# GRU recurrence: the work behind the z gate done by halves of the features

## The chip, the cores and the metric

The kernel runs on one core of a Trainium2 chip. A core has five engines with queues of their own: PE (TensorE, matrix products; the profile lists its weight loads apart, as PEld), DVE (VectorE), ACT (ScalarE), POOL (GpSimd) and SP (SyncE, which here only issues DMAs). They are kept in step by semaphores. The metric is the device time of one launch in microseconds (us).

## The reference

`x` has the shape (16, 256, 512): 16 batches, 256 channels, 512 positions. `cond` has the shape (16, 512) and holds zeros and ones. Four stages each add their result to `x`:

1. attention over the 512 positions, masked by `cond` (8 heads),
2. a causal convolution along the channels: the 16 rows of `cond` are its 16 taps, one value per tap and feature,
3. a GRU that walks over the 256 channels as its time steps, with 512 features and `cond` as the first state,
4. a second masked attention (16 heads).

The change lies in stage 3. One time step of it is

```python
def cell(h, x):
    gi = x @ W_ih + b_ih
    gh = h @ W_hh + b_hh
    i_r, i_z, i_n = jnp.split(gi, 3, axis=-1)
    h_r, h_z, h_n = jnp.split(gh, 3, axis=-1)
    r = jax.nn.sigmoid(i_r + h_r)
    z = jax.nn.sigmoid(i_z + h_z)
    n = jnp.tanh(i_n + r * h_n)
    h_new = (1.0 - z) * n + z * h
    return (h_new, h_new)
```

Each step needs the state of the step before it, so the 256 steps can't be reordered. The kernel computes the last line as `h + (1 - z) * (n - h)`.

## The kernel before

All data are fp32. `P` is 128, `B` is 16 (batches), `D` is 256 (time steps here) and `T` is 512 (features), so `NT = T // P` is 4 blocks of 128 features. The first attention ends with its sums in `xT` (128 features on the partitions, then 4 blocks, 16 batches, 256 steps), and the last attention begins when the recurrence has ended.

**State.** The new state of each step is kept in `hist`, two tiles of 16 steps each, laid out as 128 partitions x step x 4 blocks x 32. Of the 32 columns one step fills 16, even steps one half and odd steps the other; the rest is zero. `state(t)` (L1036) gives the part that a step writes and the whole slot that the next step's products read.

**Products.** `state_part` (L1080) multiplies the state by the hidden weights `whh` for one gate: for each block `f` of 128 input features, outermost, four products that stand side by side on four groups of 32 PE columns. Each product reads `slot[:, f]`, the state of one block. The profile shows 32 matmul records for one call, eight for each `f`. The input's share of r and z (`input_part`, L1058) is accumulated into the same PSUM tiles ahead of time, two steps at once, and the input's share of n is made by `turned_part` (L1066) into `turned`. PSUM holds two sets of `pr`, `pn`, `pz`; a set serves two steps and then gets the biases copied in again (L1164, ACT).

**One step** (`step`, L1094) is a chain over three engines. PE makes `pr`; ACT takes the sigmoid (`r`, L1108); DVE transposes it in blocks of 32 x 32 (`rT`, L1109), which brings the features onto the partitions. PE makes `pn`; DVE transposes that (`hT`, L1111), multiplies (`rn`, L1112) and adds the input's share (`pre`, L1113). PE makes `pz`; ACT takes the tanh of `pre` (`nn`, L1115); DVE transposes `pz` (`zT`, L1116); ACT makes `1 - z` from it (`omz`, L1117, sigmoid with scale -1); DVE makes `d = nn - h` (L1118), `m = d * omz` (L1119) and the new state `m + h` (L1120, written to `hist`). `mine` picks the 16 of 32 columns that belong to this step. A transposed tile has 128 columns: 4 blocks of 32, so its first 64 columns belong to blocks 0 and 1.

**Order of the work.** The whole recurrence is emitted in program order under a manual schedule (L1132): every engine executes its instructions in the order in which the Python lines emit them, and the framework adds the semaphores. Behind each `step(t)` the loop at L1156 emits, in this order: four input products (PE), in odd steps the three bias copies (ACT), one piece of `turned_part` (PE, with an ACT instruction in every fourth), in four steps of sixteen a copy `xw` (L1056, ACT), and two pieces of other work on DVE. The latter are convolution products for later steps (`conv`, L533) or, twice at the start of each sixteen steps, `add_part` (L1092), which adds finished states to `xT`. So on DVE two pieces of this work stand between the new state and the next step's `rT`; on PE input products stand between `pz` and the next step's `pr`.

Of the kernel before, what the change touches and what calls it, by code (L numbers as in the profile page):

```python
# [11 lines left out]
AF = mybir.ActivationFunctionType  # L12
ALU = mybir.AluOpType
# [3 lines left out]
P = 128  # L17
# [233 lines left out]
def tile_kernel(ctx: ExitStack, tc: tile.TileContext, x, cond, Wq0, Wo0, W_ih, W_hh, b_ih, b_hh,  # L251
                Wq3, Wk3, Wv3, b3, consts, out, cols):
    nc = tc.nc
    inp = x
    KC = D // P
    NT = T // P
# [768 lines left out]
    with ExitStack() as es:  # L1025
# [10 lines left out]
        def state(t):  # L1036

            slot = hist[t // PART % 2][:, t % PART]
            at_col = B * ((t + 1) % 2)
            return slot[:, :, at_col : at_col + B], slot  # L1040
# [39 lines left out]
        def state_part(slot, ps, g):  # L1080

            for f in range(NT):
                for j in range(4):
                    nc.tensor.matmul(ps[32 * j : 32 * j + 32].rearrange("p (f i) -> p f i", i=32), lhsT=slot[:, f],  # L1084
                                     rhs=gates(whh, f, j)[:, g], start=False, stop=(f == NT - 1), skip_group_check=True)
# [8 lines left out]
        def step(t):  # L1094
            pr, pn, pz = sets[t // 2 % 2]
            before, slot = state(t - 1)
            after, _ = state(t)

            def mine(tl):
                return tl.rearrange("p (f r) -> p f r", r=2 * B)[:, :, B * (t % 2) : B * (t % 2) + B]  # L1100

            def sbuf(name, shape):
                return gp.tile(shape, F32, tag=name, name=f"{name}_{t}")

            r, rT, hT, zT = (sbuf(n, [P, P]) for n in ("r", "rT", "hT", "zT"))
            rn, pre, nn, omz, d, m = (sbuf(n, [P, NT, B]) for n in ("rn", "pre", "nn", "omz", "d", "m"))
            state_part(slot, pr, GATE_R)
            nc.scalar.activation(r, pr, AF.Sigmoid)  # L1108
            nc.vector.transpose(rT, r)  # L1109
            state_part(slot, pn, GATE_N)  # L1110
            nc.vector.transpose(hT, pn)  # L1111
            nc.vector.tensor_tensor(rn, mine(hT), mine(rT), ALU.mult)  # L1112
            nc.vector.tensor_tensor(pre, rn, turned[t // PART][:, :, t % PART], ALU.add)  # L1113
            state_part(slot, pz, GATE_Z)
            nc.scalar.activation(nn, pre, AF.Tanh)  # L1115
            nc.vector.transpose(zT, pz)  # L1116
            nc.scalar.activation(omz, mine(zT), AF.Sigmoid, scale=-1.0)  # L1117
            nc.vector.tensor_tensor(d, nn, before, ALU.subtract)  # L1118
            nc.vector.tensor_tensor(m, d, omz, ALU.mult)  # L1119
            nc.vector.tensor_tensor(after, m, before, ALU.add)  # L1120

        wnats = [load_square(gw, w, n + "nat", t) for w, n, t in ((Wq3, "wq3", wqT), (Wk3, "wk3", woT), (Wv3, "wv3", None))]

# [8 lines left out]
        with tc.manual_schedule(engines=ENG):  # L1132
# [23 lines left out]
            for t in range(D):  # L1156
                step(t)
                p, q = divmod(t, PART)
                if t + 2 < D:
                    for f, g in xparts[4 * (t % 2) : 4 * (t % 2) + 4]:  # L1160
                        input_part(t // 2 + 1, f, g)
                    if t % 2:
                        for i, ps in enumerate(sets[t // 2 % 2]):
                            nc.scalar.copy(ps, bias[:, i])  # L1164
                if p + 1 < D // PART:
                    turned_part(p + 1, q)
                if p + 2 < D // PART and q >= 12:
                    take(p + 2, q - 12)
                for _ in range(2):
                    if added // 2 < p:  # L1170
                        add_part(*divmod(added, 2))
                        added += 1
                    elif taps:
                        conv(*taps.pop(0))
                if t == 8:
                    for wnat, flat, name in zip(wnats, (wq3T, wk3T, wv3T), ("wq3", "wk3", "wv3")):
                        projection(psw, wnat, flat, None, R3, DK3, name)
# [399 lines left out]
```

## Time and profile before

| | |
|---|---|
| median of three timed runs | 2614.56 us (2605.72 to 2616.25) |
| profiled execution, its own time | 2617.86 us |
| its span, first to last instruction | 2616.1 us |
| mean granted PE clock | 0.977 |
| PE busy in the span | 2448.6 us (94%) |
| DVE busy | 1780.2 us (68%) |
| ACT busy | 1016.1 us (39%) |
| POOL busy | 385.3 us (15%) |
| one DVE transpose, 128 x 128 (rT, hT, zT) | 311, 315, 318 ns |
| one DVE tensor_tensor, 128 x 64 (d, m, hist) | 225 to 226 ns |
| one ACT activation, 128 x 64 (nn, omz) | 257, 256 ns |
| one convolution product, 128 x 512 (L533) | 749 ns |

How to read it: a group of instructions is named by its line, its engine, and what it writes and reads (`hist<-m,hist` is the state's last addition). The busy time of PE includes matmuls that overlap each other, with ends that are modelled, so a high share doesn't by itself mean that PE is the limit. An engine's idle time is put down to the instruction that released it.

### The profile page before, as it was taken

Reading aid. Unit: us, or ns where it says so; the run is one execution under the profiler, and the core shown is the slowest. Engines: PE = TensorE matmul, PEld = TensorE weight load, DVE = VectorE, ACT = ScalarE, POOL = GpSimd, SP = SyncE. Lnnn points to the kernel's source line nnn. Section 1 sums busy time; section 2 is a strip of 40 time slices with the busy share of each in tenths; the row PEclk is TensorE's granted clock in tenths of the full one; section 3 lists DMA queues with packets and bytes.
Section 4 is the critical chain, followed back from the end, with each engine's and each line's share of the span. In section 5 each row is a group of like instructions: output and inputs, shape, how many; then the busy total and the mean of one; then the engine's idle time right before and its main releaser. Section 6 shows DMA issues by size and latency. Waiting matters only on the chain.

```text
span 2616.1 us, 100684 instructions
## 1 busy us (share of the span) xinstructions
PE 2448.6 (94%) x45506; PEld 1635.2 (63%) x45506; DVE 1780.2 (68%) x3810; ACT 1016.1 (39%) x2459; POOL 385.3 (15%) x382
## 2 busy tenths in 40 slices
PE   5999889959999999999999999789999999999995
PEld 3545444437888888888888888644444444444442
DVE  1578778866888888888888655455666566665652
ACT  2444444422333333333333332234444544555452
POOL 2333231210000000000000000132223222231113
PEclk9999999979999999999999999989999999999997
DMA  5222221130000000000000000010011100110001
GB/s 178 69 65 68 62 63 35 35 137 3 5 4 4 5 4 4 4 5 4 4 4 5 5 4 4 5 49 28 28 32 36 41 29 28 33 39 26 19 19 36
DMA packets 54738, 80.22 MB, mean 31 GB/s; under 512 B 15824, under 2 KB 33434, under 8 KB 54292
## 3 DMA queue, kind: packets, MB, share of 16 engines
q1 hardware_dynamic: 45076, 56.66, 7.1%
q0 software_dynamic: 9216, 16.96, 2.2%
q8 instruction: 360, 5.90, 1.0%
q14 instruction: 86, 0.70, 0.1%
HBM read 45.05 MB, written 36.75 MB: 31 GB/s over the span
## 4 chain that ended last, share of the span: by engine, by line
PE 80%; issue 6%; DMA 4%; DVE 4%; POOL 3%; ACT 1%; SPq 0%; POOLq 0%; another core or an unknown queue 0%; DVEq 0%; ACTq 0%
PE pr L1084 10%; PE pz L1084 9%; PE pn L1084 9%; PE sC L1461 8%; PE sC L1415 7%; PE avC L1475 5%; PE pt L1075 4%; PE pr L1063 4%; PE pz L1063 4%; PE smC L1381 4%; PE sC L1421 3%; PE avC L1479 2%; PE smA L908 2%; DMA backA<-result,goto 2%; PE smC L1351 2%
## 5 line engine op out<-in xcount | busy, mean ns | idle before, releaser
L1430 DVE TENSOR_REDUCE nmC<-sC 128x4 f32<-128x1024 f32 x256 | 301.8, 1221 | 208.5 <-PE sC L1415 206.8
L1468 ACT ACTIVATE wih<-sC 128x1024 f32<-128x1024 f32 x320 | 313.6, 1022 | 236.6 <-PE sC L1461 218.6
L1084 PE MATMUL pr<-whh,hist 128*32 128x128 f32 x8192 | 281.6, 275 | 14.2 <-DVE hist L1120 10.2
L1084 PEld LDWEIGHTS pr<-whh,hist 128*32 128x32 f32 x8192 | 218.8, 110 | 118.5 <-DVE hist L1120 51.1
L1084 PE MATMUL pz<-whh,hist 128*32 128x128 f32 x8192 | 279.6, 273 | 2.2 <-issue 2.2
L1084 PE MATMUL pn<-whh,hist 128*32 128x128 f32 x8192 | 278.9, 273 | 0.0
L533 DVE SCALAR_TENSOR_TENSOR yw<-xT,condT,yw 128x512 f32<-128x512 f32 x360 | 269.5, 749 | 6.8
L1063 PE MATMUL pr<-wih,xw 128*32 128x128 f32 x4096 | 222.6, 274 | 22.2 <-DMA wv3nat<-in_L_cond_Wv_dram 19.1
L1084 PEld LDWEIGHTS pz<-whh,hist 128*32 128x32 f32 x8192 | 237.3, 110 | 3.3 <-issue 3.0
L1084 PEld LDWEIGHTS pn<-whh,hist 128*32 128x32 f32 x8192 | 237.1, 110 | 0.1
L1461 PE MATMUL sC<-qC,kC 32*128 32x512 f32 (+1 forms) x1280 | 231.7, 632 | 0.4 <-ACT wih L1468 0.3
L1063 PE MATMUL pz<-wih,xw 128*32 128x128 f32 x4096 | 224.1, 274 | 3.7 <-issue 3.4
L1115 ACT ACTIVATE nn<-pre 128x64 f32<-128x64 f32 x256 | 65.7, 257 | 384.3 <-DVE pre L1113 377.0
L1108 ACT ACTIVATE r<-pr 128x128 f32<-128x128 f32 x256 | 71.0, 277 | 319.2 <-PE pr L1084 318.9
L881 DVE TENSOR_REDUCE whh<-smA 128x2 f32<-128x640 f32 (+2 forms) x211 | 150.2, 752 | 65.1 <-PE smA L873 46.2
L1415 PE MATMUL sC<-kC,qC 32*128 32x256 f32 x2048 | 185.5, 401 | 0.0
L297 POOL DMA_INDIRECT table<-xT,togo x128 | 133.5, 1043 | 248.2 <-DMA table<-xT,togo 169.4
L1516 POOL TENSOR_TENSOR aC<-aC,pbC 128x512 f32<-128x512 f32 x64 | 81.2, 1270 | 590.9 <-ACT wih L1468 287.7
L1075 PE MATMUL pt<-xw,wih 128*32 128x256 f32 x2048 | 166.8, 382 | 0.0
L1288 POOL MEMSET pbC<- 128x512 f32 x4 | 2.3, 625 | 1101.2 <-DVE xT L1092 1101.2
L1109 DVE STREAM_TRANSPOSE rT<-r 128x128 f32<-128x128 f32 x256 | 79.7, 311 | 118.8 <-ACT r L1108 102.4
L1415 PEld LDWEIGHTS sC<-kC,qC 32*128 32x128 f32 x2048 | 128.7, 184 | 46.2 <-issue 16.5
(178 smaller groups left out, 3853.8 us busy)
## 6 DMA issues: line engine op xcount, KB each, us to landing
xA<-in_x_dram SPq DMA_DIRECT2D x16, 512.0 KB
pbC<-sums SPq DMA_DIRECT2D x256, 32.0 KB
out_dram<-oC SPq DMA_DIRECT2D x32, 256.0 KB
table<-zeros SPq DMA_DIRECT2D x16, 320.0 KB
xsA<-table SPq DMA_DIRECT2D x16, 256.0 KB
result<-ocA SPq DMA_DIRECT2D x16, 256.0 KB
xsC<-table SPq DMA_DIRECT2D x16, 256.0 KB
wih<-in_L_cond_W_ih_dram SPq DMA_DIRECT2D x4, 768.0 KB
```

The lines of the kernel that those rows point to most:

```text
L297: nc.gpsimd.indirect_dma_start(tables[b], bass.IndirectOffsetOnAxis(togo[:, f, b : b + 1], 0), xT[:, f, b], None, bounds_check=ROOM - 1, o ...
L533: nc.vector.scalar_tensor_tensor(acc, xT[:, f, :, lo : lo + WIN], condT[:, f, k : k + 1], xT[:, f, :, t0 : t0 + WIN] if k == 0 else acc, A ...
L881: nc.vector.tensor_reduce(dst[:, lo : lo + len(some)], SM[0:n, some[0] : some[-1] + 1, 0:ROOM], AX.X, ALU.max, negate=True)
L1063: nc.tensor.matmul(sets[k % 2][0 if g == GATE_R else 2][32 * j : 32 * j + 32].rearrange("p (f i) -> p f i", i=32), lhsT=x2, rhs=gates(wih, ...
L1075: nc.tensor.matmul(ps[32 * j : 32 * j + 32], lhsT=wih[:, kc, 2 * T + fo * P + 32 * j : 2 * T + fo * P + 32 * j + 32], rhs=parts[p][:, kc]. ...
L1084: nc.tensor.matmul(ps[32 * j : 32 * j + 32].rearrange("p (f i) -> p f i", i=32), lhsT=slot[:, f], rhs=gates(whh, f, j)[:, g], start=False, ...
L1381: nc.tensor.matmul(SM[sm.i][:, 0:n], lhsT=w[:, kc, hp * P : (hp + 1) * P], rhs=X_[x_.i][:, kc, 0:n], start=(kc == 0), stop=(kc == KC - 1))
L1415: nc.tensor.matmul(S[st[j // 2].i][:, j % 2, u * 2 * P : (u + 1) * 2 * P], lhsT=Q[qt.i][R * j : R * j + R, c : c + P], rhs=K[kt.i][R * j : ...
L1430: nc.vector.tensor_reduce(dst[:, :, :, e_at + 1], S[st[jp].i].rearrange("p j (u k) -> p j u k", u=2), AX.X, ALU.max, negate=True)
L1461: nc.tensor.matmul(S[st[j // 2].i][:, j % 2, :], lhsT=K[kt.i][r, kc * P : kc * P + P] if kc < 2 else K[kt.i][r, ROOM:], rhs=Q[qt.i][r, :], ...
L1468: lambda jp=jp, st=st, e=e: nc.scalar.activation(E[e.i][:, 2 * jp : 2 * jp + 2], S[st[jp].i], AF.Exp))
L1475: nc.tensor.matmul(AV[acc.i][R * j : R * j + R, :], lhsT=V[v.i][:, kc, 8 * (g // 2) + 2 * j + q], rhs=E[e.i][:, j], start=(kc == 0), stop= ...
```

## The change

Behind the z gate four operations are cut in two, by halves of the features (blocks 0 and 1, then blocks 2 and 3): the transpose `zT`, the sigmoid `omz`, the product `m` and the new state. `d` stays whole and is emitted behind both transposes. The product and the state are emitted by halves in turn: product and state of the first half, then those of the second.

```diff
             nc.scalar.activation(nn, pre, AF.Tanh)
-            nc.vector.transpose(zT, pz)
-            nc.scalar.activation(omz, mine(zT), AF.Sigmoid, scale=-1.0)
+            halves = [slice(h * NT // 2, (h + 1) * NT // 2) for h in range(2)]
+            for h in range(2):
+                nc.vector.transpose(zT[:, h * P // 2 : (h + 1) * P // 2], pz[:, h * P // 2 : (h + 1) * P // 2])
+            for f in halves:
+                nc.scalar.activation(omz[:, f], mine(zT)[:, f], AF.Sigmoid, scale=-1.0)
             nc.vector.tensor_tensor(d, nn, before, ALU.subtract)
-            nc.vector.tensor_tensor(m, d, omz, ALU.mult)
-            nc.vector.tensor_tensor(after, m, before, ALU.add)
+            for f in halves:
+                nc.vector.tensor_tensor(m[:, f], d[:, f], omz[:, f], ALU.mult)
+                nc.vector.tensor_tensor(after[:, f], m[:, f], before[:, f], ALU.add)
```

PE's instructions, their order and all DMAs stay as they are. In `state_part` the products of `f = 0` and `f = 1` read what the first half writes, those of `f = 2` and `f = 3` what the second half writes.

## The prediction

> **What bounds the kernel now.** I read the stages first, then the waits of the recurrence, then single steps in the timeline. The stage table (columns: stretch, length, then busy time and instruction count of PE, PEld, DVE, ACT, POOL, then clock, DMA share, GB/s) cuts the span at the first and the last state update:
>
> ```profile
> 600.00:1684.00 1084.00, 1057.26 (x34504) 940.39 (x34504) 823.69 (x2457) 335.06 (x1274) 0.00 (x0) 1.00 0.02 4
> ```
>
> The recurrence is 1084 of 2616 us: 256 steps of 4.235 us. The change touches nothing else. PE looks 97% busy, but matmul records overlap, so this says little. The waits of 600 to 1600 us say more (who waited for whom: total us, times, longest):
>
> ```profile
> PEld pr L1084 <- DVE hist L1120: 44.8, 96, 0.7
> PEld pr L1084 <- issue: 42.8, 89, 0.8
> ```
>
> The first products of a step (pr) wait for the last instruction of the step before. The "issue" half is the same wait: those weight loads start 52 ns after the state's end, which is the latency of a semaphore. In undisturbed steps the first pr product comes 370 to 413 ns after the last pt product, where 136 ns is PE's own pace. So PE has about 0.23 to 0.28 us a step to give; the chain PE, r, rT, hT, rn, pre, z part, state sets the pace. Its last part in one odd step, first DVE, then ACT (start us, length us):
>
> ```profile
> 967.12 0.32 DVE L1116 STREAM_TRANSPOSE zT<-pz 128x128 f32<-128x128 f32 x1
> 967.46 0.23 DVE L1118 TENSOR_TENSOR d<-nn,hist 128x64 f32<-128x64 f32 x1
> 967.82 0.23 DVE L1119 TENSOR_TENSOR m<-d,omz 128x64 f32<-128x64 f32 x1
> 968.08 0.22 DVE L1120 TENSOR_TENSOR hist<-m,hist 128x64 f32<-128x64 f32 x1
> 968.22 0.74 DVE L533 SCALAR_TENSOR_TENSOR yw<-xT,condT 128x512 f32<-128x512 f32 x1
> ```
> ```profile
> 967.17 0.26 ACT L1115 ACTIVATE nn<-pre 128x64 f32<-128x64 f32 x1 [1.52 <-DVE pre L1113]
> 967.53 0.26 ACT L1117 ACTIVATE omz<-zT 128x64 f32<-128x64 f32 x1
> ```
>
> See two things. m waits for omz, not for d (d ends at 967.69, m starts at 967.82, 33 ns after omz). And L533, which depends on nothing here, starts before hist ends. By the records (medians), from the end of pre to the end of the state takes 1.163 us in even steps and 1.225 in odd ones, where nn and omz each have a second semaphore to wait for (+0.06). From there to the first product: 0.145 us into an odd step, 0.054 into an even one. Periods are 4.075 and 4.217.
>
> **The change, part by part.** Added per step: one transpose, one sigmoid, one multiply, one add; no DMA, no PE work. A half costs less than the whole, but more than half of it. I put time 0 at the end of pre.
>
> Durations. TENSOR_TENSOR: 225 ns at 64 columns, 148 at one column; the line between gives 186 at 32, and the page "VectorE: DVE Perf Modes" of the Trainium skill (section "The TRN2 errata": (N+151)/0.96 for such an add, which gives 224 at 64) gives 191; I take 0.191. Transpose of 64 columns: no row. From below, half of 318 is 159; from above, 318. It streams columns as the adds do, at about 1 per ns: 318 − 67 = 0.251. Sigmoid of 32 columns: 0.23 (257 at 64; it limits nothing below).
>
> Gaps. Dependent instructions on DVE follow after 34 ns. Independent ones start 83 ns before the end of the one ahead (hist to L533, 168 times; rT to hT, start to start 228 ns of 304). Here a rule of the skill speaks against the change: the same page, "The DRAIN you can't avoid", has the next operation start only when the pipeline is empty, and advises few operations (elsewhere it allows that one that nothing holds starts earlier). By that, every added instruction costs its full length plus a gap (priced as a rival below). I go by the row of this trace: −83 ns.
>
> A wait with two semaphores. m needs d (DVE) and omz (ACT); the trace shows a separate semaphore instruction ahead of m. Where omz was long done, m still started 104 ns after d (five steps), not 34:
>
> ```profile
> 1052.71 0.23 DVE L1118 TENSOR_TENSOR d<-nn,hist 128x64 f32<-128x64 f32 x1 [0.31 <-ACT nn L1115]
> 1053.04 0.23 DVE L1119 TENSOR_TENSOR m<-d,omz 128x64 f32<-128x64 f32 x1
> ```
>
> Even step: zT first half 0.037 to 0.288; second half starts 0.251 − 0.083 later, 0.205 to 0.456; d, now behind two transposes, 0.373 (before: 0.324) to 0.599. omz first half ends at 0.288 + 0.034 + 0.23 = 0.55, before d: **d is late next**, in place of omz. First m: 0.599 + 0.104 = 0.703 to 0.894; first half of the state 0.928 to 1.119. Before: 1.163. Gain 0.044.
> Odd step: nn ends at 0.351, so d runs 0.383 to 0.609, m 0.713 to 0.904, state half 0.938 to 1.129. Before: 1.225. Gain 0.096.
>
> Second half: m starts 0.191 − 0.083 after the first state half's start, 1.04 to 1.23; state 1.265 to 1.455. PE asks for it at f = 2, behind four groups of products of 0.109 us: after an odd step the first product is at 1.129 + 0.054, the load of f = 2 at about 1.183 + 0.436 − 0.109 = 1.51; the state is visible at 1.455 + 0.052 = 1.507. Covered, just; after an even step by 0.15. Without cover each 10 ns would cost 1.3 us over 128 steps. I charge 1 us.
>
> Sum of the clean steps: 128 × (0.044 + 0.096) = **−17.9 us**.
>
> What queues behind. On DVE two convolution products (0.75 each) follow the state; they now start at 1.37 instead of 1.08, +0.29, and stand ahead of the next rT. They end at 2.90, so rT comes at 2.82 against 2.71 (even) or 2.64 (odd) at its earliest: 0.11 to 0.18 late. It may be about 0.37 late before hT (which waits for pn anyway) is held. In one step of 16 two add_part (1.1 each) stand there; that slack is used up already:
>
> ```profile
> 678.17 2.12 DVE L1092 TENSOR_TENSOR xT<-yw,hist 128x512 f32<-128x512 f32 x2
> 680.20 0.30 DVE L1109 STREAM_TRANSPOSE rT<-r 128x128 f32<-128x128 f32 x1
> 680.43 0.30 DVE L1111 STREAM_TRANSPOSE hT<-pn 128x128 f32<-128x128 f32 x1
> ```
>
> There hT moves back by the 0.29 instead of forward by 0.044: 15 × 0.335 = **+5.0**. On ACT the bias copies and xw copies follow the second omz, about 0.08 later; r needs ACT only 1.9 us later: nothing, and at most that 0.08 in the 64 steps with an xw copy, 5 us, if r were held. In 26 steps the trace shows the first product set by PE, not by the state; there the gain of 0.07 is lost: **+1.9**.
>
> Sum: −17.9 + 5.0 + 1.9 + 1 = **−10 us**. The profiled execution took 2617.86 (span 2616.1, 1.8 around it), above the three timed runs (median 2614.56); its sum is 2608. I apply the difference to the median: **2604 us**, −0.4%. From no change this kernel can be told apart at about 0.5%.
>
> **Rivals.**
> *The extra wait of m costs 34 ns, not 104* (d late, the wait already served). For: in most steps that instruction is hidden and its price unseen. Against: the five steps. Then 2 × 0.07 × 128 = 17.9 more: 2586. The same direction if the half transpose is nearer 159 (even steps only).
> *The halves don't free the first products*: the wait is for the whole slot. PE starts at 1.45 instead of 1.163 and 1.46 instead of 1.225: 128 × 0.52 = 67, to 2681. Against: at the first step the pr loads of f = 1, 2, 3 each waited for the DMA of their own rows of whh, so waits go by region, not by tile. This is also the case that the change doesn't do what it says.
> *The other side: DVE doesn't overlap.* Place: between the two transposes and d. With a gap g between independent instructions the even state half ends at 1.285 + 2g, the odd one likewise once d is held by the transposes; before, the pair made 2.388. It decides at g = −0.045: above that the kernel is slower. At +0.034, 1.353: 128 × 0.318 = 41, and the convolution would end at 3.37, rT 0.45 late, hT 0.23: 60 more, to about 2715. Against: all pairs seen at −83.
> *The slack of rT is smaller than I think*: the +0.29 then reaches hT in common steps too; 0.05 a step takes the 10 us away and brings 2617, 0.13 brings 2638.
>
> **How the numbers follow.** Likeliest 0.60, 2604, own range 2590 to 2617 (half transpose 0.23 to 0.29, second half late by up to 0.03, the spread of the runs): 0.24 of it below 2601.5, 0.35 within 0.5%, 0.01 above. Cheap wait 0.14: faster. Slack of rT 0.08: 0.03 same, 0.05 slower. Whole slot 0.10 and no overlap 0.08: slower. So faster 0.38, same 0.38, slower 0.24. The range takes the first three, 0.82: 2578 (2586 less half the runs' spread) to 2640; it leaves out the last two.
>
> **What would show it.** Right: pr waits for the first of two hist instructions, 52 ns after it; d ends after the first omz, m 0.10 after d; pre to first state half 1.12 in both parities; convolution 0.29 later after pre; hT held only behind add_part. Wrong: transposes apart by 34 ns; a PE wait within pr at f = 2; DVE idle before hT gone; rT following L533 without a gap and hT late in common steps.

## The result, and the profile after

The changed kernel takes 2601.43 us (median of 11 runs, 2598.19 to 2606.69), the kernel before 2609.93 us (11 runs). The ratio is 0.9957, with a 95% interval from 0.9946 to 0.9968: faster by 0.4%, which is 11 us by the ratio (8 to 14 by its interval); the two medians are 8.5 us apart. The forecast was 10 us less. Its 2604 us came out 2.6 too high, since the median of three runs that it started from was itself 4.6 us above the median of eleven.

The stage table of the changed kernel (stretch, length, busy time and instruction count of PE, PEld, DVE, ACT, POOL, then clock, DMA share, GB/s), cut at the first and last state update:

```profile
597.00:1669.00 1072.00, 1044.40 (x34504) 941.72 (x34504) 869.55 (x3224) 357.78 (x1529) 0.00 (x0) 1.00 0.02 4
```

The recurrence fell from 1084 to 1072 us, though DVE has 46 us more work in it and ACT 23. One odd step on DVE, with the next step's weight loads (PEld) among it (start us, length us; `x2` merges two instructions):

```profile
959.32 0.38 DVE L1120 STREAM_TRANSPOSE zT<-pz 128x64 f32<-128x64 f32 x2
...
959.66 0.23 DVE L1123 TENSOR_TENSOR d<-nn,hist 128x64 f32<-128x64 f32 x1
...
959.99 0.19 DVE L1125 TENSOR_TENSOR m<-d,omz 128x32 f32<-128x32 f32 x1
...
960.22 0.19 DVE L1126 TENSOR_TENSOR hist<-m,hist 128x32 f32<-128x32 f32 x1
...
960.32 0.18 DVE L1125 TENSOR_TENSOR m<-d,omz 128x32 f32<-128x32 f32 x1
960.46 0.38 PEld L1084 LDWEIGHTS pr<-whh,hist 128*32 128x32 f32 x16 [0.38 <-DVE hist L1126]
...
960.54 0.19 DVE L1126 TENSOR_TENSOR hist<-m,hist 128x32 f32<-128x32 f32 x1
960.65 0.74 DVE L533 SCALAR_TENSOR_TENSOR yw<-xT,condT 128x512 f32<-128x512 f32 x1
```

The two transposes together take 0.38 us, where one took 0.32. The next step's weight loads start at 960.46, right after the first half of the state (960.22 + 0.19) and before the second half has even begun at 960.54. PE doesn't stop at `f = 2`: the products there come 109 ns after the group before, which is PE's own pace.

The waits (who waited for whom: total us, times, longest) show what that did to DVE, before and after:

```profile
DVE hT L1111 <- PE pn L1084: 61.0, 240, 1.1
```
```profile
DVE hT L1111 <- PE pn L1084: 35.1, 165, 1.1
```

DVE's idle time before `hT` was 61.0 us in 240 steps and is 35.1 in 165 now, because `rT` comes later and ends closer to it. PE waits less for the state. Its weight loads for `pr`, before and after (busy us, mean ns of one | idle us before them, and what ended most of it):

```profile
L1084 PEld LDWEIGHTS pr<-whh,hist 128*32 128x32 f32 x8192 | 218.8, 110 | 118.5 <-DVE hist L1120 51.1
```
```profile
L1084 PEld LDWEIGHTS pr<-whh,hist 128*32 128x32 f32 x8192 | 220.7, 110 | 98.7 <-issue 43.9
```

The idle time ahead of them fell by 19.8 us, while the recurrence fell by 12: a part of what the chain gave up came back as gaps elsewhere on PE. More on that below.

### The profile page after: what moved, and what is told of

It reads as the page before. It is cut to its first block, busy times and chain, and to the rows that moved or that the text cites. A ratio compares the mean times of both kernels' runs of the same rounds, so it can differ in the third digit from the quotient of the medians.

```text
span 2599.5 us, 101708 instructions
## 1 busy us (share of the span) xinstructions
PE 2433.5 (94%) x45506; PEld 1633.6 (63%) x45506; DVE 1825.4 (70%) x4578; ACT 1038.4 (40%) x2715; POOL 384.9 (15%) x382
## 4 chain that ended last, share of the span: by engine, by line
PE 75%; issue 7%; DVE 7%; DMA 5%; POOL 4%; ACT 1%; SPq 0%; DVEq 0%; POOLq 0%; ACTq 0%
PE pr L1084 9%; PE pz L1084 8%; PE pn L1084 8%; PE sC L1467 8%; PE sC L1421 7%; PE avC L1481 5%; PE pt L1075 4%; PE smC L1387 4%; PE pr L1063 4%; PE pz L1063 4%; PE sC L1427 3%; PE avC L1485 2%; DMA backA<-result,goto 2%; PE smC L1357 2%; PE smA L908 2%
## 5 line engine op out<-in xcount | busy, mean ns | idle before, releaser
L1063 PEld LDWEIGHTS pr<-wih,xw 128*32 128x32 f32 x4096 | 141.0, 110 | 28.2 <-issue 27.6
```

Source lines behind the costliest of these rows:

```text
L1063: nc.tensor.matmul(sets[k % 2][0 if g == GATE_R else 2][32 * j : 32 * j + 32].rearrange("p (f i) -> p f i", i=32), lhsT=x2, rhs=gates(wih, ...
```

## The experiments

All are compared with the kernel before in the same session. "Clean step" means the median period of even or odd steps from the end of one first-written state to the next; before it is 4.075 and 4.217 us, in the changed kernel 3.983 and 4.124. "Longer steps" are those that take more than that; the steps behind `add_part` are counted apart, and one step near the start, some 9 to 11 us longer in every run, is left out.

**Product and state by halves alone.**

```diff
-            for h in range(2):
-                nc.vector.transpose(zT[:, h * P // 2 : (h + 1) * P // 2], pz[:, h * P // 2 : (h + 1) * P // 2])
-            for f in halves:
-                nc.scalar.activation(omz[:, f], mine(zT)[:, f], AF.Sigmoid, scale=-1.0)
+            nc.vector.transpose(zT, pz)
+            nc.scalar.activation(omz, mine(zT), AF.Sigmoid, scale=-1.0)
```

> The transpose zT and the sigmoid omz are whole again; only the product m and the new state go by halves. If the gain is the earlier end of the first half of the state, then from the durations of the two traces: the first m starts 0.033 us after the whole omz as before, and the first half of the state ends 2 x 0.034 = 0.068 us earlier than the whole state did (1.095 and 1.157 us after pre in even and odd steps). 256 x 0.068 = 17.4 us gained, less 15 x 0.31 = 4.7 behind add_part and some 2.7 where PE sets the pace: about 2600 us, ratio 0.996, level with the full change. If the halves of the z part are what counts, most of the gain is gone: ratio 0.999 or more.

Measured: 2599.11 us, ratio 0.9958 (0.9944 to 0.9971). Clean steps take 4.009 and 4.149 us, 0.066 and 0.068 less than before; the first half of the state ends 1.097 and 1.155 us after `pre`. The first theory holds to 2 ns: the gain needs only the halved product and state, and this kernel is as fast as the full change with two instructions a step more than before, not four.

**Transpose and sigmoid by halves alone.**

```diff
-            for f in halves:
-                nc.vector.tensor_tensor(m[:, f], d[:, f], omz[:, f], ALU.mult)
-                nc.vector.tensor_tensor(after[:, f], m[:, f], before[:, f], ALU.add)
+            nc.vector.tensor_tensor(m, d, omz, ALU.mult)
+            nc.vector.tensor_tensor(after, m, before, ALU.add)
```

> The other half of the change alone: zT and omz by halves, m and the state whole. m then waits for the second omz, which ends 0.68 us (even) and 0.73 us (odd) after pre instead of 0.65 and 0.71. The state ends 0.04 and 0.02 us later than before: 128 x 0.06 = 8 us slower, 2618 us, ratio 1.003. If the shorter transposes and sigmoids were a gain in themselves, the ratio would be under 0.998.

Measured: 2617.76 us, ratio 1.0035 (1.0022 to 1.0049). The state ends 1.200 and 1.247 us after `pre`, against 1.163 and 1.225 before. Here, cutting two operations in two without a reader that starts on the first half was a loss of some 8 us: `m` waits for the second `omz`, which ends later than the whole one did.

**The second half first.** The changed kernel, with PE asking for the halves in the other order:

```diff
-            for f in range(NT):
+            for f in (2, 3, 0, 1):
...
-                                     rhs=gates(whh, f, j)[:, g], start=False, stop=(f == NT - 1), skip_group_check=True)
+                                     rhs=gates(whh, f, j)[:, g], start=False, stop=(f == 1), skip_group_check=True)
```

The second pair of lines only moves the mark of the last product to the block that is now last.

> The changed kernel, with the products of a step in the order f = 2, 3, 0, 1: the first products now need the second half of the state. If the first half's early end is what gains, PE starts after the second half, 1.40 and 1.46 us after pre, against 1.163 and 1.225 before: 256 x 0.235 = 60 us slower than before, about 2668 us, ratio 1.022. If it did not matter which half PE waits for (the wait being for the whole slot, or PE late for another reason), it stays at 2601.

Measured: 2662.71 us, ratio 1.0211 (1.0191 to 1.0231). In its timeline the loads start right behind the second half of the state (980.65 + 0.19), 0.38 us after the first half ended:

```profile
980.32 0.19 DVE L1126 TENSOR_TENSOR hist<-m,hist 128x32 f32<-128x32 f32 x1
...
980.65 0.19 DVE L1126 TENSOR_TENSOR hist<-m,hist 128x32 f32<-128x32 f32 x1
...
980.89 0.70 PEld L1084 LDWEIGHTS pr<-whh,hist 128*32 128x32 f32 x28 [0.71 <-DVE hist L1126]
```

With the profile after, where the loads start before the second half has begun, this shows that the waits go by region: each product waits for the half that it reads. The rival of the whole slot falls, and this is about what it would have cost: a clean step of 4.311 and 4.451 us.

**add_part on another engine.** The changed kernel with the one line of `add_part` moved:

```diff
-            nc.vector.tensor_tensor(dst, yw[p // 2 % 3][:, :, :, lo + q : lo + PART : 2], src, ALU.add)
+            nc.gpsimd.tensor_tensor(dst, yw[p // 2 % 3][:, :, :, lo + q : lo + PART : 2], src, ALU.add)
```

> The changed kernel with add_part on POOL, which is idle in the recurrence. If the change loses 15 x 0.34 us because it pushes add_part into the next step's rT and hT, the step after each add_part falls from 4.46 to 4.12 us and the kernel gains 5 us over the change: 2596 us, ratio 0.994 to the kernel before. If POOL's reads and writes disturb DVE, or a DVE instruction comes to wait for POOL, it stays at 2601 or goes above.

Measured: 2617.82 us, ratio 1.0036 (1.0022 to 1.0049), a miss by 22 us. The part that was aimed at came true: the step behind add_part fell from 4.46 to between 4.12 and 4.20 us. But in two other steps of each sixteen, as long as there are convolution products, the period rose by some 1.2 to 1.5 us, 24 steps in all. DVE, then POOL, in one of them:

```profile
868.64 0.19 DVE L1126 TENSOR_TENSOR hist<-m,hist 128x32 f32<-128x32 f32 x1
868.75 3.04 DVE L533 SCALAR_TENSOR_TENSOR yw<-xT,condT,yw 128x512 f32<-128x512 f32 x2
871.72 0.30 DVE L1109 STREAM_TRANSPOSE rT<-r 128x128 f32<-128x128 f32 x1
```
```profile
868.92 2.33 POOL L1092 TENSOR_TENSOR xT<-yw,hist 128x512 f32<-128x512 f32 x1 [60.27 <-DVE hist L1126]
```

While POOL adds, the pair of convolution products takes 3.04 us instead of 1.53. `rT` waits for that pair, and the profile has DVE busy through it. The pair is not slowed evenly. The first product is under way when POOL begins and keeps its 0.74 us. The second takes 2.23 to 2.26 us instead of 0.75, and ends 0.54 to 0.55 us after POOL's addition in all 24 cases: it looks held until POOL is done. POOL's addition takes up to 2.33 us there. Behind the last convolution product the same addition, with none beside it, takes 1.87:

```profile
1482.56 1.87 POOL L1092 TENSOR_TENSOR xT<-yw,hist 128x512 f32<-128x512 f32 x1 [61.20 <-DVE hist L1126]
```

So POOL loses about 0.45 us and DVE 1.5. The two seem to take turns rather than share; what they take turns at isn't shown here.

**Where the rest of the gain went.** By the traces the changed kernel's clean steps gain 23.7 us (sum of the clean periods 1057.3 to 1033.6) and the steps behind add_part lose 4.7 (0.8 to 5.4 us above a clean step). That leaves 19 us, of which 12.7 arrived in the recurrence. The other 6 us are in the longer steps (14.6 us in all before, 20.5 after). Ahead of more than half of these the profile shows PE with gaps inside the input products. To see whether PE is the cause, three kernels leave those products out (the input's share of r and z is missing from their result), so PE has time to spare in every step:

```diff
-                    for f, g in xparts[4 * (t % 2) : 4 * (t % 2) + 4]:
-                        input_part(t // 2 + 1, f, g)
```

The kernel before, without them:

> The kernel before without the input's products for r and z inside the loop over the steps (that share of the two gates is left out of the result): PE has 0.87 us a step more to spare, so it is never late for the state. Base for the next two. The clean steps keep 4.075 and 4.217 us, since the state sets them; only the steps lengthened by PE get shorter: about 2600 us, ratio 0.996.

Measured: 2598.31 us, ratio 0.9950 (0.9936 to 0.9963). Clean steps 4.075 and 4.216 us, as with the products. The longer steps fell from 14.6 us in all to 1.7, so nearly all of that needs the input products.

The changed kernel, without them:

> The changed kernel without the same products. In its trace the clean steps gained 0.096 us each, 24.5 us in all, and the 15 steps behind add_part lost 5 us, yet the whole gained only 11. If the missing 8 us go where PE (its program arriving in blocks, with gaps in the input products) sets the pace and no longer hides behind the wait for the state, they come back here: 19.5 us below the kernel before without the products, about 2581 us, ratio of the two 0.9925. If they go elsewhere (DVE, ACT, chance of one profile), the distance stays at 11 us, ratio 0.9957.

Measured: 2579.97 us, ratio 0.9882 (0.9866 to 0.9898), so 18.3 us below the kernel before without them, ratio of the two 0.993. The recurrence of the two, before and changed, in the stage table:

```profile
598.70:1667.90 1069.20, 831.96 (x26408) 712.86 (x26408) 823.56 (x2456) 330.61 (x1274) 0.00 (x0) 1.00 0.01 3
```
```profile
596.40:1645.40 1049.00, 830.68 (x26408) 711.92 (x26408) 866.78 (x3223) 354.05 (x1529) 0.00 (x0) 1.00 0.01 4
```

20.2 us apart, where the real kernels are 12 apart. The longer steps fell from 20.5 us to 1.5. With PE out of the way the 19 us of the chain arrive whole.

Product and state by halves alone, without them:

> Product and state by halves, zT and omz whole, without the same products. Its clean steps gain 0.068 us each, 17.4 in all, less 4.6 behind add_part: 12.8 us below the kernel before without the products, 2587 us. If PE's pace is what made it level with the full change, it is now 7 us slower than the full change; otherwise the two stay level.

Measured: 2586.77 us, ratio 0.9907 (0.9890 to 0.9924), 6.8 us above the full change without the products. So the halves of the z part are worth 7 us where PE has time, and nothing in the real kernel: its longer steps sum to 14.6 us with product and state halved and to 20.5 with all four, which takes 6 of those 7 us back.

**A version that beats both: nn and d by halves too.**

Against the kernel before:

```diff
-            nc.scalar.activation(nn, pre, AF.Tanh)
-            nc.vector.transpose(zT, pz)
-            nc.scalar.activation(omz, mine(zT), AF.Sigmoid, scale=-1.0)
-            nc.vector.tensor_tensor(d, nn, before, ALU.subtract)
-            nc.vector.tensor_tensor(m, d, omz, ALU.mult)
-            nc.vector.tensor_tensor(after, m, before, ALU.add)
+            halves = [slice(h * NT // 2, (h + 1) * NT // 2) for h in range(2)]
+            z0, z1 = (slice(h * P // 2, (h + 1) * P // 2) for h in range(2))
+            f0, f1 = halves
+            for f in halves:
+                nc.scalar.activation(nn[:, f], pre[:, f], AF.Tanh)
+            nc.vector.transpose(zT[:, z0], pz[:, z0])
+            for f in halves:
+                nc.scalar.activation(omz[:, f], mine(zT)[:, f], AF.Sigmoid, scale=-1.0)
+                if f is f0:
+                    nc.vector.tensor_tensor(d[:, f0], nn[:, f0], before[:, f0], ALU.subtract)
+                    nc.vector.transpose(zT[:, z1], pz[:, z1])
+            nc.vector.tensor_tensor(m[:, f0], d[:, f0], omz[:, f0], ALU.mult)
+            nc.vector.tensor_tensor(d[:, f1], nn[:, f1], before[:, f1], ALU.subtract)
+            nc.vector.tensor_tensor(after[:, f0], m[:, f0], before[:, f0], ALU.add)
+            nc.vector.tensor_tensor(m[:, f1], d[:, f1], omz[:, f1], ALU.mult)
+            nc.vector.tensor_tensor(after[:, f1], m[:, f1], before[:, f1], ALU.add)
```

> The changed kernel with nn and d by halves too, in the order zT first half, d first half, zT second half, m, d second half, state, m, state. The first m then waits for the first omz (0.55 + 0.033 us after pre in even steps) instead of for d: the first half of the state ends 0.06 us earlier than in the changed kernel. If the state set the pace alone, 256 x 0.06 = 15 us: 2586 us. Since PE has only 0.14 to 0.18 us left in clean steps and sets the pace in some 50 others, and DVE gets one more instruction ahead of the convolution, I expect half: 2593 us, ratio 0.9935. If PE's pace is the bound by now: 2600.

Measured: 2583.22 us, ratio 0.9891 (0.9875 to 0.9906). The first half of the state ends 1.009 and 1.071 us after `pre`, 0.06 earlier than in the changed kernel, as worked out; clean steps take 3.922 and 4.064 us. My halving of the gain for PE's pace was wrong: the longer steps sum to 18.3 us here, less than in the changed kernel, so all 15 us arrived and some more. One even step:

```profile
958.31 0.25 DVE L1120 STREAM_TRANSPOSE zT<-pz 128x64 f32<-128x64 f32 x1
958.57 0.19 DVE L1124 TENSOR_TENSOR d<-nn,hist 128x32 f32<-128x32 f32 x1
958.68 0.24 DVE L1125 STREAM_TRANSPOSE zT<-pz 128x64 f32<-128x64 f32 x1
958.87 0.19 DVE L1126 TENSOR_TENSOR m<-d,omz 128x32 f32<-128x32 f32 x1
958.98 0.19 DVE L1127 TENSOR_TENSOR d<-nn,hist 128x32 f32<-128x32 f32 x1
959.10 0.19 DVE L1128 TENSOR_TENSOR hist<-m,hist 128x32 f32<-128x32 f32 x1
```

Other instructions fill the time between `d` and `m`: `m` starts at 958.87, 0.11 after the first `d` ended at 958.76, with the transpose already under way between them. By the medians `m` still starts 104 ns after `d`, and 41 ns after the first `omz`. So it comes earlier because `d` does; the wait for `omz` that was expected to end last ends 8 ns too soon for that (33 ns behind `omz`, as in the kernel before).

## Why the prediction was right

**PE waits for the first half only.** Right: into even steps the loads start 52 ns after the first of the two state instructions, into odd steps 115 ns after it, as they did after the whole state before. With the halves asked for in the other order the kernel loses 2.1%.

**DVE overlaps independent instructions.** Right, and decisive. The two transposes start 173 ns apart, though the first takes 250. The rule that was weighed against it (the Trainium skill, "VectorE: DVE Perf Modes", "The DRAIN you can't avoid"), that the next operation starts only when the pipeline is empty, would have made the kernel about 100 us slower; the row of this trace, −83 ns, gave the right sign. The same section lets an operation that isn't held start earlier, which fits what the two transposes did.

**d is late next, and m pays 104 ns.** Right in what it costs: `m` starts 104 ns after `d` in even and odd steps alike. The separate semaphore instruction stands in the trace in every step. But `d` is barely the last: the first `omz` ends 3 to 4 ns after it, not 50 ns ahead of it as forecast for even steps. That it is `d` which holds `m` shows where the two are further apart. In the kernel before, `omz` ends 95 to 99 ns after `d` and `m` starts 33 ns after `omz`; with `nn` and `d` by halves, `omz` ends 63 ns after `d` and `m` keeps its 104 ns behind `d`. The rival in which that wait costs 34 falls.

**The size in even steps.** A term too small. I had 1.119 us from `pre` to the first half; it took 1.071. In odd steps 1.129 was forecast and 1.130 measured. The cause is the length of instructions that start behind one still in flight. The second transpose took 207 ns where I had put 251 for both. `d` did have to come behind the two transposes, as forecast, 76 ns before the second one's end, but that end was earlier: `d` started at 0.342 instead of 0.373. It took 205 ns instead of 226. One even step (the last line is ACT's):

```profile
963.36 0.38 DVE L1120 STREAM_TRANSPOSE zT<-pz 128x64 f32<-128x64 f32 x2
963.66 0.20 DVE L1123 TENSOR_TENSOR d<-nn,hist 128x64 f32<-128x64 f32 x1
963.97 0.19 DVE L1125 TENSOR_TENSOR m<-d,omz 128x32 f32<-128x32 f32 x1
```
```profile
963.35 0.26 ACT L1115 ACTIVATE nn<-pre 128x64 f32<-128x64 f32 x1 [1.46 <-DVE pre L1113]
```

It was not `nn` that held `d` in even steps: `nn` ends about 51 ns ahead of it there, against 33 ns before the change and in odd steps. The clean steps gained 23.7 us, not 17.9.

**The second half is covered.** Right: no gap at `f = 2` in even or odd steps. The 1 us charged for it wasn't needed.

**The convolution moves back, and only add_part reaches hT.** Right: 0.34 us in 14 of the 15 steps (the other was already 0.8 us long and hardly changed), 4.7 us in the trace against 5.0. The clean steps kept their full gain with `rT` late by 0.10 and 0.18 us, so the slack of `rT` is at least that large, and that rival falls. With add_part gone from DVE that step was as short as a clean one, or 0.07 us longer.

**PE sets the pace in some steps.** The mechanism was right, the term too small: 1.9 us forecast, 6 measured. I had counted 26 steps in which the first product came late and taken the gain of each; the trace after has 34, and 59 steps longer than a clean one by over 30 ns instead of 46. The lateness of these first products adds up to 6.9 us before and 12.0 after, which is 5 of the 6 us. The kernels without the input products show that it is PE. Two terms were off by 6 and 4 us in opposite directions, which is why the sum of 10 stands so close to the 11 measured (12.7 in the recurrence of the two traces): by luck the total was nearer than its parts.

**Why PE has those gaps.** The traces point at its program. Each step has 272 PE records, loads and matmuls together, and from one step to the next the gaps move some eight matmul records towards the front, so they recur about every 256 records. The DMA queue of the instructions, in the recurrence of the changed kernel and of the one without the input products:

```profile
q8 instruction: 270, 4.42, 1.7%
```
```profile
q8 instruction: 207, 3.39, 1.3%
```

These are packets of 16,384 bytes, 270 for 69,008 PE records and 207 for 52,816: one for 256 records each time. And the 36 gaps of over 200 ns between two input products, or between two products of `pn` or of `pz` (28 before), all end 1.2 to 1.6 us after such a packet has landed, though a packet lands only about every 4 us. So it looks as if PE waits there for its next instructions; no run changed the blocks, so it isn't proven. It isn't settled either why this costs the full change 6 us, product and state alone nothing, and the version with `nn` and `d` halved 4. The late first products add up to 7.2 and 11.7 us in the latter two, so the difference lies in them.

## What to carry to other kernels

In a chain that goes round between engines, as here, splitting pays at the end that another engine reads first, and only if that engine's instructions are ordered so that they need the first half first; splitting the operations ahead of it pays only where they end last, and costs where their reader stays whole. Before splitting, list what is queued behind on the same engine and how late it may be: here it was fine in fifteen steps of sixteen and not in the one whose slack was already used. A gain on the chain also uncovers the stalls that the chain used to hide, so look for the steps that another engine already sets.

## What was not expected of the hardware

An instruction on DVE that starts while the one ahead is still in flight is recorded shorter: 207 ns for the second transpose against 250 for the first, 184 ns for the second product against 192 for the first, of the same size, and 205 ns for `d` in even steps against 225 in odd ones. POOL is no free place for an addition while DVE is busy with two-input instructions: side by side, one convolution product took 2.26 us instead of 0.75 and the addition 2.33 instead of 1.87, and the product ended only behind the addition.
